# Putting VectorE's small steps together in the neighbour search of a four-layer graph kernel

## The chip, the cores and the metric

The kernel runs on one NeuronCore of one Trainium2 chip. The metric is the device time of one execution in microseconds (us). The engines are called PE (TensorE, the matrix unit), PEld (its weight loads), DVE (VectorE), ACT (ScalarE), POOL (GpSimd) and SP (SyncE, which here only issues transfers). A queue name such as SPq means transfers issued by that engine.

## The reference, cut to what matters

There are 2708 nodes with 512 features, and one adjacency matrix `adj` of 2708 x 2708 in float32, of which few entries are not zero. Four layers each add a graph product to the features and normalise:

```
# layer 0
adj_hat = adj + eye;  d = 1 / sqrt(adj_hat.sum(axis=1))
x = layernorm(x + (d[:, None] * adj_hat * d[None, :] @ x) @ W.T + b)
# layer 1
head = (adj > 0);  head = head / max(sqrt(sum(head * head, -1)), 1e-12);  inc = adj + head
x = layernorm(x + (inc @ x) / inc.sum(-1))
# layer 2: attention over the non-zero entries, and a second product, both with adj
x = layernorm(x + sigmoid(attn_a * x_a + attn_b * x_b))
# layer 3
x = layernorm(x + relu(adj @ (max(sign(x), 0) @ sign(weight).T)))
```

## The kernel before, in words

Rows and columns are cut into 22 blocks of 128 (the last has 20 rows). For each block of output rows, only those nodes of the other blocks matter that have a non-zero entry there. The kernel first searches for these nodes, writes for each block a list of their numbers, and gathers their columns of `adj` (from the transposed copy `adj_t`) into packed tiles. `ROOM` gives each block a fixed number of such tiles, 98 in all. The layers then gather feature rows by the same lists and multiply them with the packed tiles. Column blocks that are taken whole are called direct (`DIRECT`, 15 blocks with one or two each, always columns 0 to 127 or 0 to 255); they are no part of the search. If a list doesn't fit its room, a flag `over` leads to a dense kernel instead; with these inputs it doesn't run.

The search is the part from `load` (L732) to the end of the loop over `turn` (L1317). It takes one row block a turn, in the order `arrival`: blocks 1 to 21, then 0. `in_order` (L641) makes each engine keep the order in which the search is written out. The blocks are searched in the groups of `GROUPS`: (1), (2,3), (4,5), (6,7,8), (9,10,11), (12,13,14), (15,16,17), (18,19,20), (21). A turn does these things, each for a block that is so many turns old:

- `load` (L732) and `load_x` (L740): SP issues the transfers of two half rows of `adj` (704 and 650 KB), of the features, and of one tile of `adj_t`, two turns ahead. The half rows have four buffers, so each load waits for those of two turns ago to be read by DVE and ACT.
- `sum_rows` (L826): ACT sums both halves.
- `degree` (L834), `root` (L845) and `inverse_root` (L852): one turn later DVE adds the halves and 1, ACT takes the square root, and DVE refines its reciprocal by four small steps on a 128x1 column (`newton_steps`, L671), which gives `dinv` of one block.
- `mark` (L871): DVE writes a 0/1 mask of the two half rows (L895), takes the block's own diagonal out of it (L901) and keeps that diagonal (L907), and zeroes the columns of direct blocks (L912). Other small steps of DVE, passed in as a list, are put between these. Then PE makes 22 small products of the mask with a table of five columns (`side_of`, L916), which count for every node the entries in the quarters of the row block (the `hits`, in PSUM).
- `own_diagonal` (L921): one turn after a block's mark, two small DVE steps write its `dia_own` and add `foreign` to its hits of its own columns. Block 1 has its own columns direct and is left out.
- `count` (L935): in the turn after the last block of a group, DVE turns the hits into kinds (L946, L950), adds four kinds up by three additions (L955, L957), and makes a running count (L963) and a table (L973), with a column of lane numbers copied in (L977).
- `count_partitions`, `steps_of`, `look_up`, `keep_looked`, `list_nodes` (L980 to L1072): PE, DVE and ACT turn the counts into the list of nodes of the group (`index`, `row_at`). For the first two groups this is done at once, for the others over the next two turns.
- `fetch` (L1091): POOL issues one gather of 128 rows from `adj_t` for each tile of the list (L1093), and after every second one a short memset as a rest (L1099), save in the last two groups.
- `transpose_x` (L1106), `keep_transposed` (L1115), `project0` (L1122): PE transposes the features of the block, ACT copies them, PE multiplies with the first weight by eight matmuls a block (L1127). `scale0` (L1132): two turns after its arrival, ACT scales the block by `dinv` and stores it in `y_rows` in HBM.
- `fold` (L1140), `grow0` (L1152): three turns after its arrival, DVE adds the block's own share to the features (L1144, L1148) and PE adds its share to the product of block 0 (L1155).

After the search, layer 0 begins: POOL gathers rows of `y_rows` by the lists (L626) in the same queue, behind the last gather of `fetch`, and PE multiplies them with the packed tiles (L1393). The written order of a turn, with the lines that the change touches:

```
each(degree, at - 1)
each(root, at - 1)
chain(steps_of, 2)
each(sum_rows, at)
each(keep_transposed, at - 1)
steps = inverse_root(arrival[at - 1]) if 0 < at <= NTURN else []
...
if found_in:
    steps.insert(0, lambda: count(found_in))
if 0 < at <= NTURN:
    steps.insert(0, lambda: own_diagonal(arrival[at - 1]))
...
    mark(arrival[at], steps)
```

Of the kernel before, what the change touches and what calls it, by code (L numbers as in the profile page):

```python
# [19 lines left out]
P = 128  # L20
# [487 lines left out]
def sparse_layers(ctx, tc, x, adj, adj_t, w0_t, b0, w_sa, a_sa, w_gcnb, b_gcnb, wa, ba, wb, bb, w3_t,  # L508
# [75 lines left out]
    def side_of(b: int):  # L584
        return sides[:, ways.index(SPLIT[b]), :]
# [22 lines left out]
    def own_by_itself(b: int) -> bool:  # L608
        return b not in direct(b)
# [61 lines left out]
    def newton_steps(dst, v, r0, r1, n: int):  # L671
        def square():
            if n == 1:
                nc.vector.scalar_tensor_tensor(r1, r0, v, r0, op0=ALU.mult, op1=ALU.mult)
            else:
                nc.vector.tensor_tensor(r1, r0, v, op=ALU.mult)
                nc.vector.tensor_tensor(r1, r1, r0, op=ALU.mult)

        return [
            lambda: nc.vector.reciprocal(r0, r0),  # L680
            square,
            lambda: nc.vector.tensor_scalar(r1, r1, -0.5, 1.5, op0=ALU.mult, op1=ALU.add),
            lambda: nc.vector.tensor_tensor(dst, r0, r1, op=ALU.mult),
        ]
# [34 lines left out]
    with tc.tile_pool(name="s_pre", bufs=1) as pre:  # L719
# [83 lines left out]
        for b in range(NB):  # L803
# [7 lines left out]
        nc.gpsimd.iota(lane_i, pattern=[[0, KINDS * GM]], base=0, channel_multiplier=1)  # L811
        lane = pre.tile([P, KINDS * GM], BF16, name="s_lane")
        nc.vector.tensor_copy(lane, lane_i)
        lane_f = pre.tile([P, 1], F32, name="s_lane_f")
        nc.vector.tensor_copy(lane_f, lane_i[:, 0:1])
        near = pre.tile([P, KINDS - 1, NB], BF16, name="s_near")
        nc.vector.tensor_scalar(near, reach, lane_f, None, op0=ALU.is_gt)
        foreign = pre.tile([P, len(ways), KINDS - 1], F32, name="s_foreign")
        nc.vector.tensor_scalar(
            foreign, sides[:, :, : KINDS - 1], 2.0, 2.0, op0=ALU.mult, op1=ALU.add  # L820
        )
        keep = pre.tile([P, KINDS * GM, NB], BF16, name="s_keep")
        nc.vector.memset(keep, 1.0)
        nc.vector.memset(keep[:, :, 0:1], 0.0)
# [6 lines left out]
                    unused[:m, : ar.shape[1]], ar, AF.Copy, accum_out=row_sums[:m, b, h : h + 1]  # L831
                )

        def degree(b: int):  # L834

            m = rows(b)
            deg = small.tile([P, 1], F32, tag="deg", name=f"deg{b}")
            nc.vector.scalar_tensor_tensor(  # L838
                deg[:m], row_sums[:m, b, 0:1], 1.0, row_sums[:m, b, 1:2], op0=ALU.add, op1=ALU.add
            )  # L840
            degree_of[b] = deg

        degree_of = {}

        def root(b: int):  # L845
            m = rows(b)
            deg = degree_of[b]
            root_ = small.tile([P, 2], F32, tag="root", name=f"root{b}")
            nc.scalar.activation(root_[:m, 0:1], deg[:m], AF.Sqrt)
            degree_of[b] = (deg, root_)  # L850

        def inverse_root(b: int):  # L852
            m = rows(b)
            deg, root_ = degree_of.pop(b)
            return newton_steps(
                dinv[:m, b : b + 1], deg[:m], root_[:m, 0:1], root_[:m, 1:2], 1
            )

# [12 lines left out]
        def mark(b: int, others):  # L871

            others = iter(others)

            def other():
                next(others, lambda: None)()

            g = group_of[b]  # L880
            i = g.index(b)
            m = rows(b)
            if i == 0:
                find = ps_s.tile([P, D], F32, tag="find", name=f"find{b}", bufs=2)
                n = len(g)
                search[g] = {
                    "hits": find[:, : n * NB * KINDS].rearrange(
                        "p (g s c) -> p g s c", g=n, c=KINDS
                    ),
                    "before": find[:, D - n * KINDS :],  # L890
                    "diff": find[:, : n * NT * KINDS],
                }
            mask = masks[arrival.index(b) % 2]
            for ar, c0 in zip(arows[b], (0, CUT)):
                nc.vector.tensor_scalar(  # L895
                    mask[:m, c0 : c0 + ar.shape[1]], ar, 0.0, None, op0=ALU.not_equal
                )
                other()
                own = b * P - c0
                if own_by_itself(b) and 0 <= own < ar.shape[1]:  # L900
                    nc.vector.scalar_tensor_tensor(  # L901
                        mask[:m, b * P : b * P + m], ar[:, own : own + m], 0.0, off_dia[:m, :m],
                        op0=ALU.not_equal, op1=ALU.mult,
                    )
                    other()
                    scr = pre.tile([P, P], F32, tag="dia", name=f"dia{b}", bufs=1)
                    nc.vector.scalar_tensor_tensor(  # L907
                        scr[:m, :m], ar[:, own : own + m], 1.0, ident[:m, :m],
                        op0=ALU.mult, op1=ALU.mult, accum_out=dia[:m, b : b + 1],
                    )  # L910
            for j in direct(b):
                nc.vector.memset(mask[:m, j * P : (j + 1) * P], 0.0)  # L912
            for step_ in others:
                step_()
            for s in range(NB):
                nc.tensor.matmul(  # L916
                    search[g]["hits"][:, i, s, :], mask[:m, s * P : (s + 1) * P], side_of(b)[:m],
                    start=True, stop=True,
                )

        def own_diagonal(b: int):  # L921

            if b and own_by_itself(b):
                g, m = group_of[b], rows(b)
                nc.vector.scalar_tensor_tensor(
                    dia_own[:m, b : b + 1], search[g]["hits"][:m, g.index(b), b, KINDS - 1 :], 0.0,
                    dia[:m, b : b + 1], op0=ALU.is_equal, op1=ALU.mult,
                )

                own = search[g]["hits"][:m, g.index(b), b, : KINDS - 1]  # L930
                nc.vector.tensor_tensor(
                    own, own, foreign[:m, ways.index(SPLIT[b]), :], op=ALU.add
                )

        def count(g):  # L935
            b0_, G = g[0], len(g)
# [14 lines left out]
                narrow4, narrow4,  # L951
                near[:, :, b0_ : b0_ + G, None].to_broadcast([P, KINDS - 1, G, NB]), op=ALU.mult,
            )
            some = pre.tile([P, GM * NB], BF16, tag="some", name=f"some{b0_}", bufs=1)[:, :n]
            nc.vector.tensor_tensor(some, kind[:, 0], kind[:, 1], op=ALU.add)  # L955
            for c in range(2, KINDS - 1):
                nc.vector.tensor_tensor(some, some, kind[:, c], op=ALU.add)  # L957
# [14 lines left out]
            table = pre.tile([P, KINDS * GM, NT], BF16, tag="table", name=f"table{b0_}", bufs=1)  # L972
            nc.vector.tensor_tensor(  # L973
                table[:, : KINDS * G, :NB], turns,
                kind.rearrange("p c (g s) -> p (c g) s", g=G), op=ALU.mult,
            )
            nc.vector.tensor_copy(table[:, : KINDS * G, NB + 2], lane[:, : KINDS * G])  # L977
            search[g].update(table=table)

        def count_partitions(g):  # L980

# [6 lines left out]
        def steps_of(g):  # L988

            b0_, G = g[0], len(g)  # L990
            n = KINDS * G
            table, diff = search[g]["table"], search[g]["diff"]
# [12 lines left out]
            search[g]["base"] = base  # L1005
# [253 lines left out]
        def each(action, at: int):  # L1259
            if 0 <= at < NTURN:  # L1260
                action(arrival[at])

        def turn(at: int):
# [3 lines left out]
                if step_of.get(since, SOON) != SOON:  # L1267
                    action(step_of[since])

            each(degree, at - 1)  # L1270
            each(root, at - 1)
            chain(steps_of, 2)
            each(sum_rows, at)
            each(keep_transposed, at - 1)
            steps = inverse_root(arrival[at - 1]) if 0 < at <= NTURN else []
# [4 lines left out]
            if 0 < at <= NTURN:  # L1280
                steps.insert(0, lambda: own_diagonal(arrival[at - 1]))
            if at < NTURN and arrival[at]:
                mark(arrival[at], steps)
            else:
# [945 lines left out]
```

## Time and profile before

| | us |
|---|---|
| median of 3 runs | 988.28 (986.34 to 994.11) |
| the profiled execution, its own time | 992.0 |
| its span, from the first to the last instruction | 990.3 |
| search, to the first gather of layer 0 | 199.63 |
| busy over the whole span: PE, DVE, ACT, POOL | 860.8, 654.7, 381.1, 549.4 |
| DVE's L895 (masks), 42 in all | 39.5 |
| POOL's L1093 (gathers of adj_t), 98 in all | 111.3 |

The profile is that of one execution, 992.0 us long. A line of the view by stages gives the length of a stage, the busy time and number of instructions of each engine, the granted clock of PE (1.00 is full speed), the share of time that the DMA engines were busy and the rate. A line of the order of time gives the start, the duration, the engine, the line of the code, the operation, what it writes and reads, and in brackets how long the engine was idle before it and what released it. A line of the groups gives the count, the busy time in us, the mean in ns and the idle time before the group. A line of the waits gives the sum, the number and the longest. DVE instructions overlap a little: the next one often starts before the last one's end is shown. POOL's gathers are shown with the time of their issue, not that of the transfer.

### The profile page before, as it was taken

The page shows a single profiled execution, that of the slowest core. Times are in us where ns is not written, and L with a number is a line of the kernel's source. Part 1 is how long each engine was busy: PE and PEld are TensorE (multiplying, and loading weights), DVE is VectorE, ACT ScalarE, POOL GpSimd, SP SyncE. Part 2 cuts the span into 40 slices and gives each one's busy share as a digit, 9 for nine tenths or more (in the row PEclk, how much of TensorE's full clock was granted, in tenths as well). Part 3 has the DMA queues.
Part 4 walks back from the last instruction along what each step waited for, and adds up shares of the span by engine and source line. Part 5 has one row for each costly group of instructions (what it writes and reads, how often), then busy time and mean ns, then how long its engine had stood idle before and what let it go on. Part 6 is the DMA issues. An engine that isn't in the chain of part 4 may idle for free.

```text
span 990.3 us, 12880 instructions
## 1 busy us (share of the span) xinstructions
PE 860.8 (87%) x3659; PEld 452.2 (46%) x3659; DVE 654.7 (66%) x2538; ACT 381.1 (38%) x822; POOL 549.4 (55%) x660
## 2 busy tenths in 40 slices
PE   1898789759979979999999989988999999599992
PEld 0444344212222324555555634543555555378771
DVE  4888888726657766565654446675888776556685
ACT  2665556100000014554544433333444333254653
POOL 2577888687877647776542054553454320066661
PEclk9998998979989989999999998998999999889996
DMA  9999996466777646777653276786777541299985
GB/s 266 339 336 306 301 310 199 142 193 192 237 211 222 207 132 195 223 220 233 183 176 121 97 249 236 257 276 216 249 274 261 174 149 47 85 316 331 308 249 173
DMA packets 93557, 220.06 MB, mean 222 GB/s; under 512 B 13660, under 2 KB 28364, under 8 KB 93476
## 3 DMA queue, kind: packets, MB, share of 16 engines
q0 software_dynamic: 43008, 127.61, 43.5%
q1 hardware_dynamic: 38520, 76.78, 22.6%
q10 hardware_dynamic: 11948, 14.76, 4.7%
q8 instruction: 31, 0.51, 0.2%
q14 instruction: 50, 0.41, 0.1%
HBM read 178.21 MB, written 31.71 MB: 212 GB/s over the span
## 4 chain that ended last, share of the span: by engine, by line
PE 68%; DVE 14%; DMA 7%; issue 5%; ACT 2%; another core or an unknown queue 2%; POOL 1%; SPq 0%; ACTq 0%; DVEq 0%; POOLq 0%
PE l L1393 17%; PE h L1619 8%; PE e L1844 7%; PE a L1844 7%; PE l L2099 4%; PE pg L1892 4%; PE pc L1892 3%; PE y L1127 3%; PE l L2138 2%; PE l L1454 2%; PE e L1652 2%; PE a L1653 2%; PE px L1953 2%; DVE s_mask L895 2%; DMA xg<-x_rows,i 2%
## 5 line engine op out<-in xcount | busy, mean ns | idle before, releaser
L1093 POOL DMA_INDIRECT a<-in_adj_t_dram,row_at x98 | 111.3, 1136 | 58.7 <-DVE deg L838 26.1
L626 POOL DMA_INDIRECT xg<-x_rows,i x98 | 95.8, 978 | 70.7 <-PE l L1393 37.1
L626 POOL DMA_INDIRECT xg<-y_rows,i x98 | 97.7, 997 | 32.6 <-issue 19.0
L1393 PE MATMUL l<-xg,a 128*32 128x512 f32 (+3 forms) x196 | 86.0, 646 | 12.6 <-DMA xg<-y_rows,i 12.6
L1820 POOL DMA_INDIRECT xg<-x_rows,i x60 | 59.1, 986 | 61.8 <-ACT ae L1575 16.3
L1127 PE MATMUL y<-s_w,xt 128*128 128x512 f32 (+1 forms) x176 | 91.3, 667 | 1.7 <-ACT xt L1119 1.7
L626 POOL DMA_INDIRECT xg<-xw_rows,i x70 | 71.3, 1018 | 38.7 <-issue 15.9
L1820 POOL DMA_INDIRECT a<-x_rows,i x38 | 36.9, 970 | 95.1 <-DVE mask L1578 37.1
L1619 PE MATMUL h<-s_wsa,xt 128*128 128x256 f32 (+3 forms) x352 | 81.9, 385 | 0.0
L1619 PEld LDWEIGHTS h<-s_wsa,xt 128*128 128x128 f32 (+1 forms) x352 | 63.9, 186 | 24.8 <-ACT xt L1614 9.2
L830 ACT ACTIVATE unused<-arow 128x1408 uint8<-128x1408 f32 (+3 forms) x44 | 58.3, 1325 | 3.0 <-DMA x_rows<-s_zero 2.0
L663 ACT ACTIVATE rsqs<-mv 128x1 f32<-128x1 f32 (+2 forms) x56 | 11.3, 202 | 120.7 <-DVE mv L692 58.8
L1844 PE MATMUL a<-xg,a 128*32 128x512 f32 (+2 forms) x120 | 51.2, 629 | 4.3 <-DMA xg<-x_rows,i 4.3
L1127 PEld LDWEIGHTS y<-s_w,xt 128*128 128x128 f32 (+1 forms) x176 | 35.6, 213 | 41.9 <-issue 39.6
L2099 PE MATMUL l<-ws,pw 128*128 128x512 f32 (+1 forms) x210 | 50.8, 394 | 1.7 <-issue 1.2
L1844 PE MATMUL e<-xg,ae 128*32 128x512 f32 (+2 forms) x120 | 47.9, 601 | 1.1 <-issue 1.1
L694 POOL TENSOR_TENSOR rs<-mv,s_neg_half 128x1 f32<-128x1 f32 (+1 forms) x22 | 13.0, 592 | 61.4 <-DVE mv L692 52.0
L1892 PE MATMUL pg<-s_wg,pt 128*128 128x256 f32 (+1 forms) x176 | 45.0, 397 | 1.3 <-ACT pt L1880 1.3
L688 DVE BATCH_NORM_STATS2 st<-t 128x6 f32<-128x512 f32 (+1 forms) x66 | 45.3, 687 | 0.3
L916 PE MATMUL find<-s_sides,s_mask 128*128 128x5 bf16 (+1 forms) x462 | 15.7, 166 | 34.1 <-DVE s_mask L912 25.2
L2099 PEld LDWEIGHTS l<-ws,pw 128*128 128x128 f32 (+1 forms) x210 | 39.4, 190 | 11.9 <-issue 2.9
L1393 PEld LDWEIGHTS l<-xg,a 128*32 128x32 f32 (+3 forms) x196 | 19.8, 146 | 54.4 <-issue 38.6
(307 smaller groups left out, 1995.5 us busy)
## 6 DMA issues: line engine op xcount, KB each, us to landing
arow<-in_adj_dram SPq DMA_DIRECT2D x21, 704.0 KB
arow<-in_adj_dram SPq DMA_DIRECT2D x21, 650.0 KB
x_rows<-f SPq DMA_DIRECT2D x40, 256.0 KB
aw<-in_adj_t_dram SPq DMA_DIRECT2D x21, 320.0 KB
y_rows<-yt ACTq DMA_DIRECT2D x20, 256.0 KB
x_rows<-h SPq DMA_DIRECT2D x19, 257.0 KB
f<-in_x_dram SPq DMA_DIRECT2D x19, 256.0 KB
h_own<-x_rows SPq DMA_DIRECT2D x19, 256.0 KB
```

What stands on the lines that cost most here:

```text
L626: nc.gpsimd.indirect_dma_start(out=t, out_offset=None, in_=src[:, :], in_offset=bass.IndirectOffsetOnAxis(ap=index[b][:, i : i + 1], axis=0),)
L688: nc.vector.bn_stats(st[:m], t[:m])
L830: nc.scalar.activation(unused[:m, : ar.shape[1]], ar, AF.Copy, accum_out=row_sums[:m, b, h : h + 1])
L895: nc.vector.tensor_scalar(mask[:m, c0 : c0 + ar.shape[1]], ar, 0.0, None, op0=ALU.not_equal)
L1093: nc.gpsimd.indirect_dma_start(out=packed[b][:, t + len(direct(b)), :], out_offset=None, in_=adj_t, in_offset=bass.IndirectOffsetOnAxis(ap ...
L1127: nc.tensor.matmul(ps[:m], xt[:, k, :m], w0[:, k, :], start=(k == 0), stop=(k == KC - 1))
L1393: nc.tensor.matmul(ps[r0:r1], weights, moving, start=(i == order[0]), stop=last_of(b, i, order))
L1619: nc.tensor.matmul(ps, xt[:, k, :m], w[:, k, :], start=(k == 0), stop=(k == KC - 1))
L1820: nc.gpsimd.indirect_dma_start(out=g, out_offset=None, in_=x2_rows[:, :], in_offset=bass.IndirectOffsetOnAxis(ap=index[b][:, t : t + 1], a ...
L1844: nc.tensor.matmul(ps[r0:r1], weights, moving, start=(i == order[0]), stop=last_of(b, i, order))
L1892: nc.tensor.matmul(ps, pt[:, k, :m], w[:, k, :], start=(k == 0), stop=(k == KC - 1))
L2099: nc.tensor.matmul(whole[b], p[:r, h, b * P : (b + 1) * P], g[:r, :], start=(j == 0 and h == 0), stop=(j == NB - 1 and h == 1),)
```

## The change

Five things are changed, all in the search and all on DVE:

1. The degrees and inverse roots of two blocks are taken together: `degrees` works on two columns, in every second turn, for the two blocks that arrived before it. The last two blocks (21 and 0) are done alone, as before. For the first block of a pair the root comes one turn later than before, in the turn in which `scale0` uses it. With two columns, the refinement has five steps, since the square is made by two products (`newton_steps` with n = 2).
2. `own_diagonals` does the own columns of a whole group by two steps, just ahead of `count`. Their place in PSUM has a constant stride. `foreign` is laid out by block for this, in twelve small preparations instead of one.
3. The masks of direct columns are neither computed nor zeroed; the products of `mark` for these columns read a tile of zeros, `s_no_marks`, instead.
4. The three additions of kinds become one `tensor_reduce`, and `some` becomes float32.
5. The table is one tile for all groups, with the lane column written once.

```diff
+        table = pre.tile([P, KINDS * GM, NT], BF16, name="s_table")
+        nc.vector.tensor_copy(table[:, :, NB + 2], lane)
...
+        foreign = pre.tile([P, NB, KINDS - 1], F32, name="s_foreign")
+        b = 0
+        while b < NB:
+            end = next((c for c in range(b, NB) if SPLIT[c] != SPLIT[b]), NB)
+            nc.vector.tensor_scalar(
+                foreign[:, b:end],
+                side_of(b)[:, None, : KINDS - 1].to_broadcast([P, end - b, KINDS - 1]),
+                2.0, 2.0, op0=ALU.mult, op1=ALU.add,
+            )
+            b = end
+        no_marks = pre.tile([P, P], BF16, name="s_no_marks")
+        nc.vector.memset(no_marks, 0.0)
...
-        def degree(b: int):
-        def root(b: int):
-        def inverse_root(b: int):
+        def degrees(bs):
+            b, n, m = bs[0], len(bs), rows(bs[0])
+            deg = small.tile([P, 2], F32, tag="deg", name=f"deg{b}")[:m, :n]
             nc.vector.scalar_tensor_tensor(
+                deg, row_sums[:m, b : b + n, 0], 1.0, row_sums[:m, b : b + n, 1],
+                op0=ALU.add, op1=ALU.add,
+            )
+            root_ = small.tile([P, 2, 2], F32, tag="root", name=f"root{b}")
+            nc.scalar.activation(root_[:m, 0, :n], deg, AF.Sqrt)
             return newton_steps(
+                dinv[:m, b : b + n], deg, root_[:m, 0, :n], root_[:m, 1, :n], n
+            )
+        def due_degrees(at: int):
+            if at == NTURN or at == NTURN - 1:
+                return (arrival[at - 1],)
+            return tuple(arrival[at - 2 : at]) if 0 < at < NTURN and at % 2 == 0 else ()
...
+            lead = len(direct(b)) * P
             for ar, c0 in zip(arows[b], (0, CUT)):
+                skip = 0 if c0 else lead
                 nc.vector.tensor_scalar(
-                    mask[:m, c0 : c0 + ar.shape[1]], ar, 0.0, None, op0=ALU.not_equal
+                    mask[:m, c0 + skip : c0 + ar.shape[1]], ar[:, skip:], 0.0, None,
+                    op0=ALU.not_equal,
                 )
...
-            for j in direct(b):
-                nc.vector.memset(mask[:m, j * P : (j + 1) * P], 0.0)
             for s in range(NB):
+                marks = no_marks if s * P < lead else mask[:, s * P : (s + 1) * P]
                 nc.tensor.matmul(
-                    search[g]["hits"][:, i, s, :], mask[:m, s * P : (s + 1) * P], side_of(b)[:m],
+                    search[g]["hits"][:, i, s, :], marks[:m], side_of(b)[:m],
                     start=True, stop=True,
                 )
-        def own_diagonal(b: int):
+        def own_diagonals(g):
+            b0_, G, m = g[0], len(g), rows(g[0])
+            if own_by_itself(b0_):
+                own = search[g]["find"][:, b0_ * KINDS : (b0_ + G * (NB + 1)) * KINDS]
+                own = own.rearrange("p (g q) -> p g q", g=G)
...
+                nc.vector.tensor_tensor(own, own, foreign[:m, b0_ : b0_ + G, :], op=ALU.add)
...
-            nc.vector.tensor_tensor(some, kind[:, 0], kind[:, 1], op=ALU.add)
-            for c in range(2, KINDS - 1):
-                nc.vector.tensor_tensor(some, some, kind[:, c], op=ALU.add)
+            nc.vector.tensor_reduce(
+                some[:, :, None], narrow_.rearrange("p c x -> p x c"), axis=AX.X, op=ALU.add
+            )
...
-            nc.vector.tensor_copy(table[:, : KINDS * G, NB + 2], lane[:, : KINDS * G])
...
-            each(degree, at - 1)
-            each(root, at - 1)
+            steps = degrees(due_degrees(at)) if due_degrees(at) else []
...
-                steps.insert(0, lambda: own_diagonal(arrival[at - 1]))
+                steps.insert(0, lambda: own_diagonals(found_in))
```

More of the change, by code (lines that the diff above doesn't have):

```diff
@@ L817, in sparse_layers @@
         nc.vector.tensor_scalar(near, reach, lane_f, None, op0=ALU.is_gt)
[L818 to L821, printed above, removed]
+        foreign = pre.tile([P, NB, KINDS - 1], F32, name="s_foreign")
[10 more added lines that the diff above has]
+        nc.vector.memset(no_marks, 0.0)
         keep = pre.tile([P, KINDS * GM, NB], BF16, name="s_keep")
@@ L832, in sum_rows @@
                 )
-        def degree(b: int):
-            m = rows(b)
-            deg = small.tile([P, 1], F32, tag="deg", name=f"deg{b}")
+        def degrees(bs):
+            b, n, m = bs[0], len(bs), rows(bs[0])
+            deg = small.tile([P, 2], F32, tag="deg", name=f"deg{b}")[:m, :n]
             nc.vector.scalar_tensor_tensor(
-                deg[:m], row_sums[:m, b, 0:1], 1.0, row_sums[:m, b, 1:2], op0=ALU.add, op1=ALU.add
-            )
-            degree_of[b] = deg
-        degree_of = {}
-        def root(b: int):
[L846 to L850, printed above, removed]
-        def inverse_root(b: int):
-            m = rows(b)
-            deg, root_ = degree_of.pop(b)
+                deg, row_sums[:m, b : b + n, 0], 1.0, row_sums[:m, b : b + n, 1],
+                op0=ALU.add, op1=ALU.add,
+            )
+            root_ = small.tile([P, 2, 2], F32, tag="root", name=f"root{b}")
+            nc.scalar.activation(root_[:m, 0, :n], deg, AF.Sqrt)
             return newton_steps(
-                dinv[:m, b : b + 1], deg[:m], root_[:m, 0:1], root_[:m, 1:2], 1
+                dinv[:m, b : b + n], deg, root_[:m, 0, :n], root_[:m, 1, :n], n
             )
+        def due_degrees(at: int):
+            if at == NTURN or at == NTURN - 1:
+                return (arrival[at - 1],)
+            return tuple(arrival[at - 2 : at]) if 0 < at < NTURN and at % 2 == 0 else ()
         masks = [pre.tile([P, NB * P], BF16, tag=f"mask{i}", name=f"s_mask{i}") for i in range(2)]
@@ L886, in mark @@
                 search[g] = {
+                    "find": find,
                     "hits": find[:, : n * NB * KINDS].rearrange(
@@ L893, in mark @@
             mask = masks[arrival.index(b) % 2]
+            lead = len(direct(b)) * P
+            assert direct(b) == tuple(range(len(direct(b))))
             for ar, c0 in zip(arows[b], (0, CUT)):
+                skip = 0 if c0 else lead
                 nc.vector.tensor_scalar(
-                    mask[:m, c0 : c0 + ar.shape[1]], ar, 0.0, None, op0=ALU.not_equal
+                    mask[:m, c0 + skip : c0 + ar.shape[1]], ar[:, skip:], 0.0, None,
+                    op0=ALU.not_equal,
                 )
@@ L915, in mark @@
             for s in range(NB):
+                marks = no_marks if s * P < lead else mask[:, s * P : (s + 1) * P]
                 nc.tensor.matmul(
-                    search[g]["hits"][:, i, s, :], mask[:m, s * P : (s + 1) * P], side_of(b)[:m],
+                    search[g]["hits"][:, i, s, :], marks[:m], side_of(b)[:m],
                     start=True, stop=True,
                 )
-        def own_diagonal(b: int):
-            if b and own_by_itself(b):
-                g, m = group_of[b], rows(b)
+        def own_diagonals(g):
[3 more added lines that the diff above has]
+                own = own.rearrange("p (g q) -> p g q", g=G)
                 nc.vector.scalar_tensor_tensor(
-                    dia_own[:m, b : b + 1], search[g]["hits"][:m, g.index(b), b, KINDS - 1 :], 0.0,
-                    dia[:m, b : b + 1], op0=ALU.is_equal, op1=ALU.mult,
-                )
[L930 to L933, printed above, removed]
+                    dia_own[:m, b0_ : b0_ + G], own[:m, :, KINDS - 1], 0.0,
+                    dia[:m, b0_ : b0_ + G], op0=ALU.is_equal, op1=ALU.mult,
+                )
+                own = own[:m, :, : KINDS - 1]
+                nc.vector.tensor_tensor(own, own, foreign[:m, b0_ : b0_ + G, :], op=ALU.add)
         def count(g):
@@ L953, in count @@
             )
-            some = pre.tile([P, GM * NB], BF16, tag="some", name=f"some{b0_}", bufs=1)[:, :n]
-            nc.vector.tensor_tensor(some, kind[:, 0], kind[:, 1], op=ALU.add)
-            for c in range(2, KINDS - 1):
-                nc.vector.tensor_tensor(some, some, kind[:, c], op=ALU.add)
+            some = pre.tile([P, GM * NB], F32, tag="some", name=f"some{b0_}", bufs=1)[:, :n]
+            nc.vector.tensor_reduce(
+                some[:, :, None], narrow_.rearrange("p c x -> p x c"), axis=AX.X, op=ALU.add
+            )
             nc.vector.scalar_tensor_tensor(
@@ L971, in count @@
             )
-            table = pre.tile([P, KINDS * GM, NT], BF16, tag="table", name=f"table{b0_}", bufs=1)
             nc.vector.tensor_tensor(
@@ L976, in count @@
             )
-            nc.vector.tensor_copy(table[:, : KINDS * G, NB + 2], lane[:, : KINDS * G])
-            search[g].update(table=table)
         def count_partitions(g):
@@ L991, in steps_of @@
             n = KINDS * G
-            table, diff = search[g]["table"], search[g]["diff"]
+            diff = search[g]["diff"]
             base = small.tile([P, 2, KINDS * GM], F32, tag="base", name=f"base{b0_}")
@@ L1274, in turn @@
             each(keep_transposed, at - 1)
-            steps = inverse_root(arrival[at - 1]) if 0 < at <= NTURN else []
             found_in = step_of.get(1)
@@ L1279, in turn @@
                 steps.insert(0, lambda: count(found_in))
-            if 0 < at <= NTURN:
-                steps.insert(0, lambda: own_diagonal(arrival[at - 1]))
+                steps.insert(0, lambda: own_diagonals(found_in))
             if at < NTURN and arrival[at]:
```

## The prediction

> **What bounds the kernel now.** I read the busy slices of the page, then the busy time by stages of 25 us, then who waited for whom on each engine between 20 and 195 us, then the instructions in order of time. The change lies in the search, from the start to about 190 us; the four layers follow from 199.6 us. By stages (the columns are length, busy us and count of PE, PEld, DVE, ACT, POOL, then PE's granted clock, DMA share, GB/s):
>
> ```profile
> 50.00:75.00 25.00, 21.94 (x134) 11.04 (x132) 22.00 (x87) 16.30 (x31) 19.98 (x22) 1.00 0.99 337
> 75.00:100.00 25.00, 20.02 (x139) 11.07 (x139) 22.29 (x77) 13.41 (x24) 17.97 (x19) 0.86 0.92 308
> 100.00:125.00 25.00, 19.40 (x136) 10.65 (x137) 20.76 (x87) 12.83 (x23) 21.27 (x25) 0.93 0.90 299
> 125.00:150.00 25.00, 21.42 (x133) 11.81 (x134) 21.21 (x82) 14.06 (x25) 21.27 (x25) 0.91 0.94 302
> 150.00:175.00 25.00, 23.26 (x133) 11.88 (x132) 20.58 (x88) 14.77 (x29) 21.42 (x24) 0.89 0.63 187
> ```
>
> Nothing is idle here: PE, DVE and POOL are each busy 78 to 93%, DMA 0.90 to 0.99 until 150 us. So the busy share doesn't name the bound; the waits do. The search ends when POOL has issued its last row gather (L1093) and the first gather of layer 0 follows at 199.63. POOL's order of time, with the idle time before an instruction in brackets:
>
> ```profile
> 46.29 1.42 POOL L1093 DMA_INDIRECT a<-in_adj_t_dram,row_at  x1 [7.84 <-DVE deg L838]
> 70.81 1.57 POOL L1093 DMA_INDIRECT a<-in_adj_t_dram,row_at  x1 [1.92 <-DVE s_own L1144]
> 93.89 1.57 POOL L1093 DMA_INDIRECT a<-in_adj_t_dram,row_at  x1 [4.54 <-DVE s_own L1144]
> ...
> 178.54 0.44 POOL L1099 MEMSET s_rest<- 128x384 f32 x1
> 182.79 1.39 POOL L1093 DMA_INDIRECT a<-in_adj_t_dram,row_at  x1 [3.82 <-DVE s_own L1144]
> ...
> 199.63 1.01 POOL L626 DMA_INDIRECT xg<-y_rows,i  x1 [0.30 <-issue]
> ```
>
> These four pauses are POOL waiting for DVE's lists of groups (2,3), (4,5), (6,7,8) and (18,19,20). From 93.89 to 178.98 POOL never pauses. Its end is thus the list of (6,7,8), plus 85.1 us of gathers, or the list of (18,19,20) if that is later, plus 16.84 us for the last twelve. DVE itself hardly waits after 46 us; the largest:
>
> ```profile
> DVE turns L1053 <- ACT look L1045: 2.6, 1, 2.6
> DVE root L680 <- ACT root L849: 2.6, 2, 1.5
> DVE table L973 <- PE l L1155: 2.4, 1, 2.4
> ```
>
> **What the Trainium skill says.** "Perfetto Trace Analysis", section Optimizing Scalar/DVE Operations: each DVE operation pays some 60 ns beside its elements, 125 ns with PSUM, and grouping helps where the engine is saturated. The trace agrees: a 128x1 step is 135 to 212 ns long. "VectorE: DVE Perf Modes", The perf-mode tier table: tensor_reduce runs only at 1x. The trace's reduce of 308 elements takes 0.48 us and of 176 takes 0.34, about one element a cycle. "DMA: Bandwidth & Descriptors", Specifications: about 358 GB/s of HBM per core. The 25 us stages stop at 339, but a 5 us window (35 to 40 us) has 397, so the figure is no hard wall here.
>
> **The change, part by part.** The rows it touches:
>
> ```profile
> L674 DVE SCALAR_TENSOR_TENSOR root<-root,deg 128x1 f32<-128x1 f32 (+1 forms) x22 | 4.7, 212 | 0.1
> L683 DVE TENSOR_TENSOR s_dinv<-root 128x1 f32<-128x1 f32 (+1 forms) x22 | 3.5, 159 | 0.8
> L931 DVE TENSOR_TENSOR find<-find,s_foreign 128x4 f32<-128x4 f32 (+1 forms) x20 | 3.4, 169 | 0.7
> L957 DVE TENSOR_TENSOR some<-some,kind 128x66 bf16<-128x66 bf16 (+2 forms) x18 | 3.4, 187 | 0.6
> L912 DVE MEMSET s_mask<- 128x64 uint32 x20 | 2.1, 112 | 0.0
> L977 DVE COPY table<-s_lane 128x15 bf16<-128x15 bf16 (+2 forms) x9 | 2.0, 219 | 0.0
> ```
>
> Neighbours on DVE overlap (a 0.15 us step often starts 0.07 before its forerunner ends), so I price by start-to-start distances.
> - Inverse roots: four dependent steps take about 0.60 us a block (at 77.47: 0.10 + 0.25 + 0.19 + 0.08). A pair has five, since the fused square becomes two products: about 0.75. 22 x 0.60 - (10 x 0.75 + 2 x 0.60) = 4.5 us. Degrees: ten fewer at 0.1: 1.0.
> - Own columns: 0.26 a block (72.18 to 72.44), 20 times, against 0.28 for eight groups: 3.0.
> - Masks: 18 zeroings after block 1's two, at 0.09 (77.57 to 77.65), 1.6; and 128 columns less for each. 1408 columns take 889 ns and 1300 take 830, 0.55 ns a column, 0.07 each: 1.3.
> - Three additions (73.83 to 74.52, 0.69) become one reduce of 264 strided elements: 0.43 by the reduces above, so 0.46 start to start; 0.23 to 0.34 a group, 2.4 in nine. The trace has no strided bf16 reduce: were it 0.3 slower, this part gives nothing (-2.4); it can't be far below.
> - The lane column written once: nine copies at 0.08, 0.7.
> - Added: eleven more preparations of foreign columns and one memset, about 0.06 to 0.1 each, 0.9 us before 5.6 us, where DVE idles 0.57 and then 3.58 us for the first rows; at most 0.5 shows, and then only if those rows come early.
>
> The sum is 14.5 us of DVE, 0.66 a turn. PE keeps its 22 find products a block (those for direct columns read a zero tile), and the orders of SP, POOL and PE are otherwise the same; no DMA is added.
>
> A new wait: the even blocks' roots come one turn later, in the turn of their scaling, so ACT's scale0 waits for DVE's last root step, which ends the mark. Behind it on ACT are only the y_rows store and sometimes keep_looked. In the longest case (turn of 71.31) ACT would scale at 78.3 instead of 74.84; but it then idles 3.68 us for DVE's next degree at 79.02, which covers this. In odd turns ACT no longer waits for a degree at all. Without that cover it would cost up to 3.5 us in each of three turns. I take zero.
>
> **The sum.** Until DVE's mask at 33.51, which waits 1.63 us for its rows, nothing is gained: the first rows and ACT's queue set that. List (2,3) then saves one root chain (0.6), its additions (0.28), its lane copy and memset: 1.0. Turns 3 to 10, to the list of (6,7,8): roots 1.8, degrees 0.4, own columns 1.25, masks 1.1, additions 0.8, lane 0.25, together 5.6; two of DVE's waits on ACT (1.11 for a root at 65.99, 0.81 for a row sum at 68.75) fall away as the root leaves that turn and the row sum moves back, and 0.35 is lost to a row sum at 91.25 that stays: about 7.2. POOL allows as much: 1.0 + (1.92 - 0.16) + (4.54 - 0.16) = 7.1. DMA may not: at 0.936 share over these 60 us, reaching 1.0 gives 3.9. I take 5.5, between. POOL then ends its run at 178.98 - 5.5 = 173.5. The list of (18,19,20), at 182.35, would gain 13.6 until 148 us by DVE alone (by the same counts 10.8 of steps to turn 17, and 3.1 of waits, less 0.35); after that the chain of waits lies on PE's projections, back to back to 174, and nothing more is gained. DMA at full share from 25 to 150 gives 125 x 0.062 = 7.7. I take 8.5, hence 173.85, and the last twelve gathers start there, 8.5 early (182.35 to 173.85) with POOL's pause gone. Layer 0 waits for POOL alone at its start (PE is idle from 192 to 204.9), y_rows are written before 190 and come earlier still, and the later orders are the same. So the profiled 992.0 us (span 990.3) become 983.5; off the median, 988.28 - 8.5 = 979.8, 0.86% less.
>
> **Rivals.**
> 1. DMA gives way (its 397 GB/s window speaks for it): all POOL's pauses after the second list go, 7.1 + 3.82 - 0.16 = 10.8, with up to 1.5 more if the first lists come earlier. 977.5, in reach of 976. Against it: share 0.99 from 50 to 75.
> 2. PE binds. After a mark PE does find, transposes, eight projections and a sum: 0.53 + 0.49 + 3.44 + 0.86 = 5.3 us, but 7.0 where the projections take 5.1 to 5.7, as at 79.66 and 148.25. Turns are 6.5 now. If about half the turns are held, half of the gain stays: 4, so 984.3. Against it: PE's waits from 20 to 195 us add up to 31 us.
> 3. Slower: ACT's late scaling delays its next row sums, which free the row buffers (SP waited 14.8 us in 12 loads for these), so rows land late. A pair of turns gains 1.3; if ACT is late by over 1.3 us a pair, the change loses. At 1.6 in ten pairs: +3, 991.3. Against it: the 3.68 us of cover.
>
> **How the numbers follow.** Chances: the forecast (6 to 9.9 us less) 0.45; rival 1 (beyond) 0.30; rival 2 (0 to 6 less) 0.20; rival 3 0.05, of which 0.03 beyond 1%. About 1%, 9.9 us, is what a measurement can tell from no change. So faster 0.30, same 0.67, slower 0.03. The forecast's own range is 978.4 to 982.3; with rivals 1 and 2, an unknown reduce of 2.4 us and three runs that span 7.8 us, 974 to 987.
>
> **What would show it.** DVE busy to 195 us about 15 us less; L838 x12, own columns x8, no L912, a reduce of 0.40 to 0.45 us. POOL's pauses before (4,5) and (18,19,20) gone, that before (6,7,8) near 2 us; the first xg gather near 191; ACT's wait for roots at scale0 not followed by a wait of the row masks. Wrong if DVE waits on arow or PE by more than 5 us in all, or if the gain at the first xg gather is not found at the end.

## The result, and the profile after

The changed kernel takes 985.0 us (median of 22 runs), the kernel before 992.32 us in the same series. The ratio is 0.9942, 95% interval 0.9924 to 0.9960: 0.58% less, some 5.7 us. The profiled execution took 988.11 us (span 986.3), that of before 992.0 (span 990.3).

The order of time of POOL in the trace after (start, duration, then in brackets the idle time before it and what ended it) answers to the list of pauses of before:

```profile
44.50 1.29 POOL L1099 DMA_INDIRECT a<-in_adj_t_dram,row_at  x1 [8.15 <-DVE deg L848]
...
67.88 0.95 POOL L1099 DMA_INDIRECT a<-in_adj_t_dram,row_at  x1 [0.16 <-DVE s_dia_own L936]
...
88.58 1.50 POOL L1099 DMA_INDIRECT a<-in_adj_t_dram,row_at  x1 [2.62 <-DVE s_own L1150]
...
135.49 1.50 POOL L1099 DMA_INDIRECT a<-in_adj_t_dram,row_at  x1 [1.04 <-DVE s_own L1150]
...
158.57 1.56 POOL L1099 DMA_INDIRECT a<-in_adj_t_dram,row_at  x1 [3.02 <-DVE s_own L1150]
...
180.06 1.40 POOL L1099 DMA_INDIRECT a<-in_adj_t_dram,row_at  x1 [5.96 <-DVE s_own L1150]
...
197.18 1.01 POOL L626 DMA_INDIRECT xg<-y_rows,i  x1 [0.30 <-issue]
```

The pause before (4,5) is gone, and (6,7,8) starts 5.3 us earlier (93.89 to 88.58). But pauses of 1.04 and 3.02 us are new before (12,13,14) and (15,16,17), that before (18,19,20) grew from 3.82 to 5.96, and this last list is only 2.7 us earlier. The gain of the first half was partly lost in the second. Layer 0 begins 2.45 us earlier (199.63 to 197.18), and the span ends 4.0 us earlier.

The stages after (PE, PEld, DVE, ACT, POOL busy, granted clock, DMA share, GB/s):

```profile
75.00:100.00 25.00, 21.54 (x131) 11.46 (x130) 22.09 (x71) 16.02 (x27) 19.42 (x22) 0.84 0.99 350
100.00:125.00 25.00, 22.59 (x155) 11.86 (x154) 20.30 (x64) 13.09 (x22) 21.27 (x25) 0.91 0.94 322
125.00:150.00 25.00, 19.82 (x140) 10.94 (x138) 18.27 (x64) 13.38 (x24) 20.53 (x25) 0.93 0.83 261
```

VectorE now has more idle time: it is busy for 18.27 of 25 us in the last of these, against 21.21 before. What it waited for between 25 and 175 us (sum, number, longest):

```profile
DVE root L680 <- issue: 5.6, 2, 4.8
DVE s_mask L904 <- issue: 4.5, 3, 2.2
...
DVE s_mask L904 <- DMA arow<-in_adj_dram: 2.6, 2, 2.0
```

The mask's 7.1 us are waits for row halves. (For the 4.5 put down to "issue": the mask starts at 149.90 and 152.91, and SP, which waits for the same two landings before it may reuse their transfer slots, goes on at 149.89 and 152.90.) The 4.8 us at the reciprocal are one event, which ended at 130.78: ScalarE waited 4.49 us before the copy of the looked-up counts, and the pair's square root stood behind that copy.

Some of the groups after (busy us, mean ns, idle before):

```profile
L964 DVE TENSOR_REDUCE some<-kind 128x66 f32<-128x264 bf16 (+2 forms) x9 | 4.5, 503 | 0.3
...
L683 DVE TENSOR_TENSOR s_dinv<-root 128x2 f32<-128x2 f32 (+2 forms) x12 | 1.9, 160 | 0.4
...
L942 DVE TENSOR_TENSOR find<-find,s_foreign 128x12 f32<-128x12 f32 (+2 forms) x8 | 1.4, 175 | 0.3
```

A step on 2 or 12 columns costs what one on 1 or 4 columns did (160 ns against 159, 175 against 169), so fewer of them is a true saving. The reduce is the exception: 4.5 us, where the three additions took 5.1.

### The profile page after: what moved, and what is told of

Its sections match the earlier page's. It is cut to its first block, busy times and chain, and to the rows that moved or that the text cites. A ratio compares the mean times of both kernels' runs of the same rounds, so it can differ in the third digit from the quotient of the medians.

```text
span 986.3 us, 12778 instructions
## 1 busy us (share of the span) xinstructions
PE 860.5 (87%) x3659; PEld 452.8 (46%) x3659; DVE 647.5 (66%) x2440; ACT 381.3 (39%) x812; POOL 546.1 (55%) x660
## 4 chain that ended last, share of the span: by engine, by line
PE 65%; DVE 6%; DMA 4%; issue 4%; POOL 2%; ACT 1%; another core or an unknown queue 1%; ACTq 0%; POOLq 0%; DVEq 0%
PE l L1396 16%; PE h L1622 8%; PE e L1847 6%; PE a L1847 6%; PE l L2102 5%; PE pg L1895 4%; PE pc L1895 3%; PE l L2141 3%; DMA xg<-x_rows,i 2%; PE e L1655 2%; PE l L1457 2%; PE a L1656 2%; PE px L1956 2%; PE xt1p L1615 1%
## 5 line engine op out<-in xcount | busy, mean ns | idle before, releaser
L1099 POOL DMA_INDIRECT a<-in_adj_t_dram,row_at x98 | 108.4, 1107 | 59.9 <-issue 21.5
L1396 PE MATMUL l<-xg,a 128*32 128x512 f32 (+3 forms) x196 | 88.0, 651 | 14.0 <-DMA xg<-y_rows,i 13.1
L904 DVE TENSOR_SCALAR s_mask<-arow 128x1300 bf16<-128x1300 f32 (+5 forms) x42 | 37.6, 900 | 9.4 <-DMA arow<-in_adj_dram 4.9
```

The source lines that it names most:

```text
L904: nc.vector.tensor_scalar(mask[:m, c0 + skip : c0 + ar.shape[1]], ar[:, skip:], 0.0, None, op0=ALU.not_equal,)
L1099: nc.gpsimd.indirect_dma_start(out=packed[b][:, t + len(direct(b)), :], out_offset=None, in_=adj_t, in_offset=bass.IndirectOffsetOnAxis(ap ...
L1396: nc.tensor.matmul(ps[r0:r1], weights, moving, start=(i == order[0]), stop=last_of(b, i, order))
```

## The experiments

There are four series of runs, each on a chip of its own. The kernel before took 963.4 to 964.9 us in all four, 28 us less than in the series of the result. Some 23 of these lie behind the first gather of layer 0 (790.7 us of the span against 767.9), at nearly the same granted clock (0.946 and 0.949); no run here shows why. So only ratios to before within a series, and differences of such ratios, are compared. The kernel before in the series of the result and its second trace below are called the first and the second trace of before, likewise for the changed kernel. The theories: V, VectorE's steps still set the pace; P, the wait that pairing brings eats the gain; B, PE or the transfers bind, and D, the transfers alone; Q, POOL's queue of gathers binds; L, row buffers come free too late; M, a mishap of one execution.

### The parts undone and alone

The unedited changed kernel again:

> The changed kernel, unedited, as the control of its batch and as a second trace. Measured so far 985.0 us, ratio 0.994. Theory P (pairing): in its first trace VectorE stood 4.8 us at the reciprocal of one pair's roots, because ScalarE was held in the copy of the looked-up counts; if this belongs to the kernel, waits of 3 us or more at that line come again and the list of (18,19,20) starts near 180 us. Theory M (mishap of one execution): the wait is gone, the list of (18,19,20) starts near 174 to 176 us.

Measured: 0.9924 (0.9894 to 0.9953), 956.92 us. The long wait at the reciprocal did not come again (0.5 us in all), and (18,19,20) starts at 171.82. M holds for that wait (the list came even earlier than its 174 to 176).

Roots of each block by themselves, as the only edit to the changed kernel:

```diff
-            if at == NTURN or at == NTURN - 1:
-                return (arrival[at - 1],)
-            return tuple(arrival[at - 2 : at]) if 0 < at < NTURN and at % 2 == 0 else ()
+            return (arrival[at - 1],) if 0 < at <= NTURN else ()
```

> The changed kernel with the roots of each block by themselves, as before; the other four parts kept. Theory V (VectorE's steps set the time, pairing included): about 5.5 us of the 14.5 are given back, so 2 to 4 us slower than the changed kernel, ratio 0.997 to 0.998. Theory P (the wait that pairing brings eats what it saves): not slower than the changed kernel, ratio 0.991 to 0.995, and the list of (18,19,20) not later than 180 us. Theory B (PE or the transfers bind the turns): ratio within 0.001 of the changed kernel, with VectorE idle for the difference.

Measured: 0.9927 (0.9905 to 0.9950). Undoing the largest part costs nothing that can be measured. Its last list needs no pause at all.

The three additions back in the place of the reduce:

```diff
-            some = pre.tile([P, GM * NB], F32, ...)
-            nc.vector.tensor_reduce(some[:, :, None], narrow_.rearrange("p c x -> p x c"), ...)
+            some = pre.tile([P, GM * NB], BF16, ...)
+            nc.vector.tensor_tensor(some, kind[:, 0], kind[:, 1], op=ALU.add)
+            for c in range(2, KINDS - 1):
+                nc.vector.tensor_tensor(some, some, kind[:, c], op=ALU.add)
```

> The changed kernel with three additions again instead of the reduce. The trace of after has the reduce of 264 elements at 0.60 us, start to start about the same as the three additions at 0.69. All theories: within 1 us of the changed kernel, ratio 0.993 to 0.996; if the reduce had been worth the forecast 2.4 us it would be 1.5 us or more slower.

Measured: 0.9914 (0.9891 to 0.9937). This is below the range forecast, but not told from the changed kernel's 0.9924: no gain of the reduce can be seen.

The pairs alone, put into the kernel before (`degrees` and `due_degrees` in place of `degree`, `root` and `inverse_root`):

> The kernel before with the paired degrees and roots alone. Theory V: 5.5 us of VectorE saved, 2.5 to 3.5 us faster, ratio 0.9965 to 0.9975. Theory P: the late scaling and the wait at the root take it, ratio 0.999 to 1.003, with waits at the reciprocal of 3 us or more. Theory B: ratio 0.998 to 1.0 without such waits.

Measured: 0.9947 (0.9927 to 0.9967), 5.1 us. V expected at most 3.5. So pairing alone brings 0.53%, the other four parts alone 0.73%, and both together 0.76%. The parts don't add (the sum, 1.26%, lies outside the interval of both together, 0.47 to 1.06%, though each part has an error of its own): something else caps the sum. P falls too, since the pairs are no loss.

### What caps it

The kernel before again, for a trace on these chips:

> The kernel before, unedited: a second trace, for its pauses of POOL. Ratio 1.0. If chip or execution alone set the pauses, they differ from the first trace by 2 us or more: there (6,7,8) began at 93.89 after a pause of 4.54 and (18,19,20) at 182.79 after 3.82. Theory Q (POOL's own queue of gathers is the floor): (6,7,8) to (18,19,20) takes at least 85.1 us again, whatever the chip.

Measured: 0.9999 (0.9982 to 1.0015). Two of the pauses of the first trace come again, a little shorter: (6,7,8) at 90.25 after 3.53, (18,19,20) at 178.89 after 2.50, the first gather of layer 0 at 194.96 (189.27 in the changed kernel's second trace). From one list to the other are 88.6 us; without the last pause 86.1, as Q has it. The pause of 1.92 us before (4,5) is not there this time, so its absence in the changed kernel can't be put down to the change.

POOL's rests taken out:

```diff
-                if group_of[b] in RESTED and fetched[0] % 2 == 0:
-                    nc.gpsimd.memset(rest, 0.0)
```

> The changed kernel without POOL's 43 rests between gathers, 0.6 us each, 26 us in all. Theory Q: from the list of (6,7,8) on POOL no longer binds, the first gather of layer 0 comes 1 to 4 us earlier, as far as the lists allow, ratio to before 0.988 to 0.992. Theory V (the lists, hence VectorE) and theory B (PE or transfers): POOL pauses longer before each list instead, and the time stays within 1 us of the changed kernel.

Measured: 0.9914 (0.9888 to 0.9941): 1.0 us better than the changed kernel, not told apart. This lies in Q's range too, and the first gather of layer 0 came 3.0 us earlier (186.25), as Q has it. But most of what the rests gave back went into pauses: 7.98 us before (6,7,8), 5.94 before (18,19,20). Both sides are seen, and this run alone doesn't decide.

`fold` left out, so that VectorE has 19 us less to do:

```diff
-            each(fold, at - 3)
```

> The changed kernel without fold: the block's own share is not added to the features in the search, which takes two steps of 0.9 us together out of VectorE in each of 21 turns, 19 us in all (the output lacks this share). Theory V: the lists come earlier by 0.9 us a turn, and the kernel is 6 to 12 us faster than the changed kernel, ratio to before 0.981 to 0.988. Theory Q: only the list of (6,7,8) and POOL's pauses can give, some 4 us in all, ratio 0.988 to 0.991. Theory B: within 1.5 us of the changed kernel, ratio 0.991 to 0.995, and VectorE's waits grow by 10 us or more.

Measured: 0.9918 (0.9886 to 0.9951). V expected 6 to 12 us and nothing came that can be told from zero. From 25 to 175 us VectorE is busy 114.01 us instead of 128.33, 14.3 less, and its wait for rows is 13.2 longer (6.4 in the changed kernel):

```profile
DVE s_mask L904 <- DMA arow<-in_adj_dram: 19.6, 11, 3.6
```

Up to 86 us, ahead of the list of (6,7,8), it is busy 7.6 us less (45.83 against 53.46 from 25 us) and waits 7.5 us longer for rows (10.3 against 2.8), and the list comes no earlier. For this stretch V falls. Behind this list the run can't test V, for POOL doesn't pause for over 0.5 us between these two lines:

```profile
88.15 1.35 POOL L1099 DMA_INDIRECT a<-in_adj_t_dram,row_at  x1 [5.09 <-DVE row_at L1078]
...
186.89 0.95 POOL L626 DMA_INDIRECT xg<-y_rows,i  x1 [0.30 <-issue]
```

Here POOL's own queue is the floor, and not only here. From the start of the list of (2,3) to layer 0:

| trace | us | pauses of POOL over 0.5 us in it |
|---|---|---|
| before, second | 149.2 | 6.0 |
| changed, second | 144.7 | 4.1 |
| separate roots | 143.4 | 2.7 |
| three additions | 142.7 | 1.8 |
| without fold | 142.3 | 5.1 |

Once (2,3) is there, earlier lists alone can gain little more than these pauses. So a cap stood close by for V, for the pairs and for the other four parts, whatever held the lists.

What VectorE saves beyond the change, it gives back waiting for row halves. Who held these rows can be read from SP, which issues them. Its waits from 25 to 175 us in the kernel before, second trace:

```profile
SPq L737 <- DVE dia L907: 35.4, 12, 4.6
SPq L737 <- DVE s_mask L895: 21.3, 15, 2.8
SPq L737 <- ACT unused L830: 16.6, 15, 2.9
...
SPq L737 <- DMA y_rows<-yt: 2.7, 1, 2.7
```

and in the changed kernel, second trace:

```profile
SPq L737 <- DVE dia L917: 19.7, 8, 4.8
...
SPq L737 <- DMA y_rows<-yt: 14.4, 5, 4.2
SPq L742 <- DMA y_rows<-yt: 9.2, 2, 5.9
SPq L743 <- DMA y_rows<-yt: 7.8, 1, 7.8
SPq L743 <- DMA arow<-in_adj_dram: 6.3, 4, 2.4
SPq L737 <- ACT unused L840: 6.0, 9, 2.9
```

Before, SP waited mostly for VectorE and ScalarE to free the buffers. After, it waits mostly for earlier transfers to land, ScalarE's stores of `y_rows` above all. The limit on the loads moved from the engines toward the transfers. Whether it is their rate or the landing of a single store isn't separated by any run: after its issue at 73.42 SP issues nothing until 81.64, waiting for a store of `y_rows` (the 7.8 us above), and from 80 to 85 us the share of DMA is only 0.77.

ScalarE's copy behind the next turn's square root:

```diff
             steps = degrees(due_degrees(at)) if due_degrees(at) else []
+            chain(keep_looked, 3)
...
-            chain(keep_looked, 2)
```

> The changed kernel with ScalarE's copy of the looked-up counts behind the next turn's square root instead of ahead of it. Theory P (the paired roots wait behind this copy): no wait of over 1 us at the reciprocal, 1 to 4 us faster than the changed kernel, ratio 0.988 to 0.992. The others: within 1 us, ratio 0.991 to 0.995.

Measured: 0.9912 (0.9885 to 0.9938), in P's range, but also within the changed kernel's interval. It can't be told from no change.

### More and fewer bytes

The features loaded a second time, in both kernels:

```diff
+            again = pre.tile([P, D], F32, tag="again", name=f"again{b}", bufs=2)
+            nc.sync.dma_start(again[:m], x[b * P : b * P + m, :])
```

> The changed kernel with each block's features loaded a second time into a tile that nobody reads: 256 KB more a turn, some 0.74 us at the 345 GB/s of the stages from 25 to 100 us. Theory D (the transfers of a turn, some 2.2 MB, set the pace once VectorE is relieved): 10 to 15 us slower than the changed kernel, ratio to before 1.002 to 1.008. Theory V (VectorE sets it): under 4 us slower, ratio below 0.997.

> The kernel before with the same second load. Theory D: the transfers bind here too now, so both kernels meet: 7 to 12 us slower than before, ratio 1.007 to 1.012, and not more than 4 us from the changed kernel with this load. Theory V: under 4 us slower, and the changed kernel keeps its lead of 7 us.

Measured: 1.0043 (1.0020 to 1.0065) for the changed kernel, 1.0060 (1.0030 to 1.0090) for the one before; 967.65 and 969.84 us. With some 11% more bytes (a turn has 1674 KB of loads, 256 of stores, and over 22 turns there are 98 gathers and 20 loads of direct columns of 64 KB, together 2273 KB a turn; 256 are added) the lead of the change falls from 0.76% to 0.17%, which the intervals don't tell from zero. For the changed kernel D holds. The load costs it 1.2% and the one before only 0.6% (5.8 us), which lies between V's under 4 us and D's 7 us or more: before had slack in its transfers, after has less.

Six row buffers, without fold:

```diff
-                ar = pre.tile([P, CUT], F32, tag="arow", ..., bufs=4)
+                ar = pre.tile([P, CUT], F32, tag="arow", ..., bufs=6)
```

> The changed kernel without fold (the output lacks that share), with six row buffers instead of four. Without fold VectorE waited 19.6 us for rows. Theory D (rate): the rows come no sooner, within 1.5 us of the kernel without fold, ratio 0.990 to 0.9935. Theory L (rows are late because their buffers come free late): the waits for rows fall below 8 us, 3 to 6 us faster, ratio 0.985 to 0.989.

Measured: 0.9905 (0.9872 to 0.9937), and VectorE still waits 19.3 us for rows. L falls.

Half of the features loaded, without fold:

```diff
-            nc.sync.dma_start(place_of_x(b)[:m, :D], x[b * P : b * P + m, :])
+            nc.sync.dma_start(place_of_x(b)[:m, : D // 2], x[b * P : b * P + m, : D // 2])
...
+        for b in arrival:
+            nc.gpsimd.memset(place_of_x(b)[: rows(b), D // 2 : D], 0.0)
```

> The changed kernel without fold and with half of each block's features loaded, the other half set to zero by POOL ahead of its first gather (the output is that of other features): 128 KB less a turn, 0.37 us at 345 GB/s. Theory D: VectorE waits 5 to 8 us less for rows than the 19.6 without fold, the list of (6,7,8) comes 2 to 4 us earlier, and as POOL then has its gathers without a pause, 2 to 4 us faster, ratio 0.987 to 0.990. Theory L: no change, 0.991 to 0.993.

Measured: 0.9882 (0.9857 to 0.9907), inside D's range, but its interval overlaps that of the kernel without fold (0.9886 to 0.9951). The wait for rows falls from 19.6 to 8.2:

```profile
DVE s_mask L906 <- DMA arow<-in_adj_dram: 8.2, 7, 3.1
```

Behind the list of (2,3) POOL has no pause left at all, and takes 142.1 us to layer 0: this is its own queue. The same half load in the two kernels, and without POOL's rests:

> The kernel before with half of each block's features loaded and the other half set to zero by POOL ahead of its first gather (the output is that of other features): 128 KB less a turn, 0.37 us at 345 GB/s. Theory D for the changed kernel says that before was held by VectorE and little by the transfers: 0 to 3 us faster than before, ratio 0.997 to 1.0. If the transfers already held before as much as after: 4 to 7 us, ratio 0.993 to 0.996.

> The changed kernel with the same half load. Theory D: its lead over before with the same load grows from 7.3 us to 9 us or more, ratio to before 0.986 to 0.990. Theory Q or PE: the lead stays at 7 us or less, ratio not below 0.990.

> The changed kernel with the half load and without POOL's rests, 26 us of POOL in all. Theory D alone: like the one with the rests, within 1.5 us. Theory Q (with fewer bytes POOL's queue is the next floor): 2 to 5 us faster than with the rests, ratio to before 0.983 to 0.987.

Measured: before 0.9991 (0.9976 to 1.0006), after 0.9893 (0.9874 to 0.9912), after without rests 0.9808 (0.9779 to 0.9838). Before gains nothing from fewer bytes, as D says of a kernel that VectorE held. The lead of the change is 0.98% by the ratios and 7.9 us by the medians (962.45 to 954.51): D's 9 us or more is neither confirmed nor refuted. Without rests 8.2 us more come off by the ratios and 10.3 by the medians (954.51 to 944.22), more than Q's 2 to 5. POOL's order of time, with the half load and rests:

```profile
85.62 1.57 POOL L1102 DMA_INDIRECT a<-in_adj_t_dram,row_at  x1 [1.43 <-DVE s_own L1153]
...
183.96 1.01 POOL L626 DMA_INDIRECT xg<-y_rows,i  x1 [0.31 <-issue]
```

and without the rests:

```profile
83.21 1.57 POOL L1102 DMA_INDIRECT a<-in_adj_t_dram,row_at  x1 [2.71 <-DVE s_own L1151]
...
175.09 1.48 POOL L626 DMA_INDIRECT xg<-y_rows,i  x1 [0.30 <-DMA s_wsa<-in_w_sa_dram]
```

In both no pause of over 0.5 us lies between the two lines: 98.3 us of queue in the first, 91.9 in the second. Rests removed under the full load bring 1.0 us by the ratios, under the half load 8.2. And without rests, the half load brings 10 us (0.9914 to 0.9808), with them 3.0 (0.9924 to 0.9893), which the intervals don't tell from zero. Two floors, transfers and POOL's queue, lie close together, and taking away one shows the other. PE is not the floor at the changed kernel's time: this last kernel runs the same products, on features of which half are zero, and reaches layer 0 at 175.09, 14.2 us before the changed kernel's second trace.

At last the late copy, the additions and six buffers together (the three edits shown above), which leaves out nothing:

> The changed kernel with ScalarE's copy behind the next square root, the three additions instead of the reduce, and six row buffers instead of four. As the transfers bind, all theories expect little: 0 to 3 us faster than the changed kernel, ratio to before 0.988 to 0.992; below 0.988 would say that late buffers matter after all.

Measured: 0.9903 (0.9886 to 0.9921), 954.35 us. It is faster than before by 0.97%; against the changed kernel (0.9924, 0.9894 to 0.9953) the intervals overlap, so it isn't shown to beat it.

## Why the prediction was right or wrong

- **The lists as gates, and the list of (6,7,8).** The gates are right. 5.5 us were forecast and 5.3 came in the first pair of traces. In the second it was 3.8 (90.25 to 86.44), near the 3.9 of the forecast's DMA term, so the close hit of the first pair is partly luck. The pause before (4,5) went as said, but it was absent in the second trace of before too.
- **The list of (18,19,20): the term that was too large.** The step that failed is "DMA at full share from 25 to 150 gives 125 x 0.062 = 7.7. I take 8.5"; the 0.8 us above its own bound have no reason given. The share did not rise to 1: it was 0.94 before and 0.92 after over this stretch in the first pair (317 and 319 GB/s), 0.94 and 0.96 in the second (324 and 332). Even with the second load it stayed at 0.97 (346). The list came 2.7 us earlier in the first pair, where the changed kernel had the 4.8 us hold at the reciprocal, and 7.1 in the second. There the last twelve gathers took 17.45 us instead of the 16.07 of before, where the forecast let them keep their length. The first gather of layer 0 thus came 2.45 and 5.7 us earlier, not 8.5. In two of the holes SP couldn't issue: in the changed kernel's second trace the share is 0.70 from 45 to 50 us, as SP has waited for VectorE's `dia` (8.0 us in two waits from 42 to 51 us, while VectorE made the list of (2,3) at once), and 0.77 from 80 to 85, in the wait for the store of `y_rows`. So the free share wasn't there for a faster VectorE to fill as the forecast took it. What would fill it stays open.
- **VectorE's sum of 14.5 us.** The parts look right, save one, if the durations are added up. By the groups of the first pair (busy, before to after): degrees and roots 17.9 to 12.2, own columns 6.4 to 3.1, masks and zeroings 41.6 to 37.6. But neighbours overlap: from 20 us to VectorE's last step of the last list, its busy time fell by 9.4 us in the first pair (141.57 to 132.18) and by 11.7 in the second (144.44 to 132.74), not by 14.5. The reduce was mis-sized: 0.65 us start to start (69.38 to 70.03) where 0.46 was taken, against 0.69 of the additions, so the forecast's lower end, nearly nothing, came true. And the sum was the wrong place to look: `no_fold` gave VectorE 14 us more and no time came of it.
- **The wait at scale0, priced at zero.** Right as far as the runs can tell: separate roots (0.9927) and the late copy (0.9912) don't differ from the changed kernel. The trace of after had a worse case, 4.8 us at the reciprocal, with the copy ahead of the root on ScalarE. In the second trace it was 0.5. What held the copy is open: PE's last small product is shown as ended at 125.96, the copy started at 130.21.
- **Kept to the end.** Right: 2.45 us at the first gather of layer 0 were 4.0 at the end of the span, 5.7 were 7.7. The part of the span behind that gather is 764 to 773 us in all 16 traces of the experiments, so the 2 us on top lie within this scatter.
- **The rivals.** The first (transfers give way) did not come: pauses of 2.04 us stay before (6,7,8) and (18,19,20) in the second trace, and the second load cost time. The second named the size, half of the gain, but the wrong cause: the transfers and POOL's queue, not PE. The third did not come.
- **The alarm.** "Wrong if DVE waits on arow or PE by more than 5 us in all" did go off: 7.1 us on rows in the first trace, 6.4 on rows and 4.8 on PE in the second.
- **The sign.** This step failed too. Likeliest was a time within 1%, on the ground that "About 1%, 9.9 us, is what a measurement can tell from no change". That ground was wrong: 22 runs of each kernel tell 0.58% with 0.18% to either side, so the change is faster, by a little. The forecast gain of 0.86% is larger than this interval allows (0.40 to 0.76%). The time itself, 985.0 us, lies within 974 to 987, but the kernel before had meanwhile moved from 988.28 to 992.32, so that this says little about the gain.

The Trainium skill's advice in "Perfetto Trace Analysis", section Optimizing Scalar/DVE Operations, that grouping helps if the engine is saturated, held with its condition: it helped while VectorE held the row buffers, and stopped where it no longer did. "DMA: Bandwidth & Descriptors", section Specifications, gives about 358 GB/s of HBM for a core; the 25 us stages of the kernels with the second load reach 321 to 369, and over 125 us they come to 346 and 351, so the figure is a fair mark for a long stage here. The 336 to 345 of the changed kernel's second trace between 25 and 125 us lie close under it.

## What to carry to other kernels

When an engine's small steps are saved, look first at who will be waited for next, and how far away that is: here the transfers were 6% from full and POOL's queue had 6 us of pauses left, so a forecast saving of 14.5 us on VectorE brought 6 to 7. To find out, free the engine of much more than the change does, and then take away bytes or queue time. Check in each trace whether the queue behind pauses at all; if it doesn't, the run can't show a gain. A part that gives next to nothing alone (rests, 1.0 us) can give 8 us once its neighbour is out of the way. Parts of a change that are each worth nearly the whole (0.53%, 0.73%, together 0.76%) are a sign of such a cap.

## What the runs showed of the hardware

- A reduce of 264 bf16 elements whose summed axis is strided took 0.60 us, of 88 elements 0.30: 1.7 ns for each further element ((0.60 - 0.30) / 176). The Trainium skill, "VectorE: DVE Perf Modes", The perf-mode tier table, has tensor_reduce at 1x only; the contiguous f32 reduces of this trace (352 elements in 0.52 us, 220 in 0.38) take 1.1 ns an element. Three bf16 additions of 66 columns each were as fast as the strided reduce.
- In the changed kernel the second load, 11% more bytes, raised the rate over 25 to 150 us from 332 to 346 GB/s and the share from 0.96 to 0.97, and cost 1.2% of the time.
